# Attention maxima turned on VectorE and carried through DRAM, in a fused transformer block on one core

## The chip, the cores and the metric

The kernel runs on one core of one Trainium2 chip. The metric is the device time of one execution in microseconds. The time of a kernel is the median of several executions. One execution is profiled by the hardware, and all the views in this document are views of that execution's trace.

The engines go by the names of the profile: PE is TensorE's matmul stream and PEld its weight loads, DVE is VectorE, ACT is ScalarE, POOL is GpSimd, SP is SyncE. SP computes nothing here: it issues nearly all DMAs, one after the other, and SPq marks its instructions.

## The reference

One block of a diffusion transformer on x of 16 batches x 256 tokens x 256 channels, with 16 heads of 16 channels each:

```
x  = x + gate_a * (softmax(q k^T * scale) v) W_proj     # self-attention of modulate(ln(x))
x  = x + (softmax(q_c k_c^T * scale) v_c) W_cproj       # cross-attention to a context of 256 tokens
x  = x + gate_m * gelu(modulate(ln(x)) W_mlp1) W_mlp2   # MLP with 1024 hidden channels
```

The shifts, scales and gates come from a conditioning vector for each batch. All is float32. What matters here is the softmax: for each head and each query token the kernel subtracts the largest score over the keys before the exponential, and the change touches the way that this maximum takes.

## The kernel before, in words

**Stages.** There are 16 self-attentions ("s") and 16 cross-attentions ("c"), 32 *units* in all (`seq`, lines 725 to 740). Five s units come first, then s and c alternate, and the last are c. A setup stage (`PRE`, line 55) comes first and the MLP last. The change lies in the attention stage, which the trace shows from about 30 to 540 us.

**A unit has eight beats**, k = 0 to 7 (`beat`, lines 984 to 1136). All instructions are emitted in the order in which `beat` writes them (`InOrder`, line 40), and each engine's queue keeps that order. In beat k of unit n, `visit` (line 962) emits two things:

- for the *next* unit n+1, one piece of the scores in the orientation that the maximum needs: `s_tile` puts four `s` matmuls on PE, and one DVE reduction `mx<-s` takes the maxima of 4 heads x 128 query tokens (lines 640 to 666). After beat 3 the maxima of the unit's first 8 heads are complete (half 0), after beat 7 those of the other 8 (half 1).
- for the *current* unit n, one pair of heads in the transposed orientation: `t_part` puts four `st` matmuls on PE (line 676), and `exp` has ACT turn them into `pt` (line 687).

**How the maximum enters.** For each pair of heads the stacked tile `u.q` has 64 rows for each of two heads, and so has `u.k`. Row 63 of `u.q` holds minus the maximum of each query token, and row 63 of `u.k` holds a constant 1 (`ones`, line 88, sent by `one_rows`, line 884). So the `st` matmul over 64 rows gives score minus maximum; the `s` matmul uses 63 rows only.

**The way of a maximum** is `m_part` (line 668), once for each half of a unit, 64 times in all. The tile `mx` has query tokens on partitions and heads along a row. PE transposes 128 x 16 of it into a PSUM bank (`psm`), ACT multiplies by -1 into `m`, and one SP DMA (`big<-m`, 16 rows of 512 bytes) writes row 63 of both heads' rows of `u.q`. Half 1 of unit n is handled in beat 0 of unit n, after the `visit`, and is needed by the `st` matmuls of beat 4. Half 0 of unit n+1 is handled in beat 4 of unit n, after the `visit`, and is needed by the first `st` matmuls of unit n+1, in its beat 0. So each half has four beats.

**What else stands in SP's queue.** In beat 0 SP sends the new high parts of k (`big<-h_k` or `h_kc`, two DMAs of 256 KB), `big<-m`, and the low part `l_k`. In beat 1 come `S` and `U`, pieces of the attention output (`pull(1)`, line 573), and then the reciprocal row sums to DRAM (`rd<-S`, `spread`, line 584). In beat 4 come `h_q` twice, `big<-m` and `l_q`. In beat 5 a context load `c` may follow, and then `back` (line 588) reads the sums back, spread over all partitions (`R<-rd`, 256 KB). In beat 6 come the gates `g` (s units), `S` and `U` again (`pull(0)`), and a store.

Of the kernel before, what the change touches and what calls it, by code (L numbers as in the profile page):

```python
# [16 lines left out]
P = 128  # L17
# [4 lines left out]
def pixart_block(  # L22
# [29 lines left out]
                return tc.keep_in_program_order(i) if self.on else i  # L52
            return issue

    E_ = {'M': ((-17, -12, -5, -1, 1), (0, 3, 4, 7, 9), (8, 11, 13, 15)), 'LN': {'s': 'pool', 'c': 'pool', 'q': 'pool'}, 'ON': (1, 1, 1), 'H': (7, 11, 14, 15), 'AP': 23, 'DV': (0, 1), 'HP': (1, 0, 2), 'W1P': [(-9, 3), (-8, 3), (-7, 3), (-6, 3), (-4, 5), (-4, 7), (-3, 1), (-3, 5)], 'W2P': [(-4, 7), (-3, 2), (-3, 4), (-3, 6), (-3, 7), (-2, 2), (-2, 4), (-2, 6), (-1, 0), (-1, 1)], 'PRE': 'z0qp z0kp load ld2 ld3 rest one0 silu b12 brow L0a turn L0b b1 L0d scale hik lok T0t z1kp b2 shift T0h T0l ldm hiq loq hiv b1 K0a K0m L1a L1b lov L2a L2b bk z1qa bq K0h K0x K0ya L1e K0l K0s Q0a Q0m Q0h Q0x Q0ya T1t Q0l Q0s T1h V0a V0b T1l bv L2c L3a L3b L3p L3c K1a K1b', 'SL': {(-1, 0): 'Q1a Q1b K1x K1y K1l K1s', (-1, 1): 'T2t T2h T2p V1a Q1x Q1y Q1l Q1s', (-1, 2): 'V1b cpm2', (-1, 3): 'rest z2ka', (-1, 4): 'M0 rest one1 ld4', (-1, 5): 'K2a vone', (-1, 6): 'K2m z2qa', (-1, 7): 'rest one2', (0, 0): 'cpm0 d2 rest', (0, 1): 'rest', (0, 4): 'rest', (1, 0): 'rest', (1, 2): 'rest', (1, 4): 'rest'}}

    PE = InOrder(nc.tensor, True)
    ACT, DVE, POOL, SP = (InOrder(e, True) for e in (nc.scalar, nc.vector, nc.gpsimd, nc.sync))
# [9 lines left out]
    def ps_gen(name, tag=None):  # L68


        if tag is None and ps_turn[0] is not None:
            ps_turn[0] ^= 1
            tag = (SHORT, LONG)[ps_turn[0]]
        tag = tag or SHORT
        return psum.tile([P, 512], F32, tag=tag, name=name, bufs=2)
# [3 lines left out]
    DVE.memset(wz, 0.0)  # L79
    ident = const.tile([P, P], F32, name="ident")  # L80
    make_identity(nc, ident)
    mhalf = const.tile([P, 2], F32, name="mhalf")
    POOL.memset(mhalf, -0.5)

# [1 line left out]
    vts = [const.tile([P, NT, NH, 32], F32, name=f"v{i}") for i in range(3)]  # L86
    wself = const.tile([P, 16, H], F32R, name="wself")
    ones = const.tile([8, N], F32, name="ones")
    DVE.memset(ones, 1.0)


    BMOD, BQKV, BQC, BKVC, BM1 = 0, 12, 18, 20, 24
# [547 lines left out]
    def s_tile(u, g, par, t, bank=None, home=sp):  # L640

        alone = bank is None
        if alone:
            turn_of_s[0] ^= 1
            bank = turn_of_s[0]
        apart = isinstance(home, tuple)
        for j in range(2):
            PE.matmul((home[bank] if apart else home[:, bank])[:, j * N:(j + 1) * N],  # L650
                      u.q[par * 64:par * 64 + 63, 2 * g + j, t * P:(t + 1) * P],
                      u.k[par * 64:par * 64 + 63, 2 * g + j, :], start=True, stop=True)
            if j == 0:
                yield
        if u.mx is None:
            u.mx = work.tile([P, 2, 2, 4, NT], F32, tag="mx", name=f"mx_{u.n}", bufs=3)
        mx = u.mx.rearrange("p f r a t -> p r f a t")
        a = slice(2 * (g % 2), 2 * (g % 2) + 2)
        if alone or apart:
            src = home[bank] if apart else sp[:, bank]  # L660
            DVE.tensor_reduce(mx[:, par, g // 2, a, t], src.rearrange("p (j n) -> p j n", j=2),
                              AX.X, ALU.max)
        elif bank == 1:
            DVE.tensor_reduce(mx[:, :, g // 2, a, t], home.rearrange("p r (j n) -> p r j n", j=2),
                              AX.X, ALU.max)
        yield

    def m_part(u, hf):

        pst = ps_gen(f"psm_{u.n}_{hf}", SHORT)  # L670
        PE.transpose(pst[:16, :P], u.mx[:, hf].rearrange("p r a t -> p (r a t)"), ident)
        m = work.tile([16, P], F32R, tag="m", name=f"m_{u.n}_{hf}", bufs=1)
        ACT.mul(m, pst[:16, :P], -1.0)
        SP.dma_start(u.q[63:P:64, 4 * hf:4 * hf + 4, :].bitcast(F32), m.bitcast(F32))

    def t_part(u, pair, par):

# [16 lines left out]
    def exps():  # L694

        for f in later:
            f()
        later.clear()
# [234 lines left out]
    for k, f in zip("abpc", (u3.ln[0].steps[0], lambda: u3.ln[0].steps[1](False), u3.ln[0].pow, u3.ln[0].steps[2])):  # L933
        word["L3" + k] = f
    word["ldm"], word["cpm0"], word["cpm2"] = f_mod_load, lambda: f_mod(0), lambda: f_mod(2)
    word["M0"] = lambda: m_part(u0, 0)
    word["rest"] = lambda: next(rest, None)
    word["vone"] = lambda: [POOL.memset(v[:, :, :, 1:2 * HD:2], 1.0) for v in vts]
    for n, f in (("load", f_load), ("silu", f_silu), ("turn", f_turn), ("brow", f_brow),
# [44 lines left out]
    def beat(n, k):  # L984
# [20 lines left out]
        if k == 6:  # L1005
            if q2 and not n:
                q2.V.keep()
            if p2 and not alone:
                p2.end()
        visit(n, k)  # L1010
        if k == 0:
            if cur:
                m_part(cur, 1)
            exps()
            if q3 and q3.ready:
                q3.T[0].place()
            if prev:
                av_part(prev, 3)
            if q3 and q3.ready:
                q3.T[0].turn((0,))  # L1020
            if q2:
                q2.K.low()
                q2.K.send_low()
            if p2:
                p2.norm()
                p2.high()
                p2.low()
        elif k == 1:
            exps()
            run(lanes(q2 and q2.Q, q2 and n and q2.V))  # L1030
            if prev:
                p1.pull(1)
            if lc:
                lc.ln[0].steps[0]()
            if lx:
                if lx.b in (0, B - 1):
                    lx.ln[1].steps[0]()
                lx.ln[1].steps[1]()
                lx.ln[1].steps[2]()
        elif k == 2:  # L1040
            exps()
            if cur:
                av_part(cur, 0)
            if q3:
                q3.T[0].turn((1,) if q3.ready else (0, 1))
            if ls:
                ls.ln[0].steps[0]()
            elif prev:
                p1.recip()
                p1.spread()  # L1050
            if not (q3 and q3.kind == "c"):
                spare(n)
        elif k == 3:
            if q3:
                q3.T[0].high()
                if q3.kind == "c":
                    q3.T[0].full()
            exps()
            if alone and p2:
                p2.proj(0)  # L1060
                p2.proj(1)
            elif n:
                run(lanes(p2, q2 and q2.Q))
            else:
                run(lanes(q2.V, q2.Q))
            if q3 and q3.kind == "s":
                q3.T[0].low()
            if prev and ls:
                p1.recip()
                p1.spread()  # L1070
        elif k == 4:
            if nxt and lx:
                m_part(nxt, 0)
            exps()
            if nxt and not lx:
                m_part(nxt, 0)
            if alone:
                p2.end()
            if cur:
                av_part(cur, 1)  # L1080
            if lx:
                lx.T[1].turn()
            if q2:
                q2.Q.low()
                q2.Q.send_low()
            if q3 and q3.kind == "c":
                q3.T[0].rest_pool()
                spare(n)
            if ls:
                ls.ln[0].steps[1]()  # L1090
                ls.ln[0].steps[2]()
                ls.ready = True
        elif k == 5:
            exps()
            run(lanes(q3 and q3.K, (None if alone else p2) if n else q2.V))
            if cur:
                o_out(cur, 0)
            if lc:
                lc.ln[0].steps[1]()
                lc.ln[0].steps[2]()  # L1100
                lc.ready = True
            v = unit(n + 5)
            if v and v.kind == "c":
                load(v)
            if prev:
                p1.back()
        elif k == 6:
            exps()
            if lx:
                lx.T[1].high()  # L1110
            if cur:
                cur.post.begin()
                av_part(cur, 2)
                cur.post.pull(0)
            if q3 and p2:
                q3.vk = lanes(q3.V, q3.K)
                run(q3.vk, 1)
            if p3:
                p3.store()
            if lx:  # L1120
                lx.T[1].full()
                lx.T[1].rest_pool()
        elif k == 7:
            exps()
            run(q3.vk if q3 and p2 else lanes(q3 and q3.V, q3 and q3.K))
            if late:
                p2.add()
                p2.added = True
            elif lc:
                lc.ln[1].steps[0]()  # L1130
            v = unit(n + 5)
            if v and v.kind == "s":
                load(v)
            if n == nu - 1:
                p2.add()
                p2.store()
# [99 lines left out]
```

## Time and profile before

| what | value |
|---|---|
| median of 3 executions (lowest, highest) | 743.61 us (742.79, 745.01) |
| the profiled execution: its own time, its span | 742.45 us, 740.7 us |
| instructions in the trace | 22556 |
| busy over the span: PE, DVE, ACT, POOL | 722.2, 569.4, 556.1, 528.5 us |
| granted TensorE clock | 0.999 |
| DMA: packets, bytes | 81388, 106.15 MB |
| of `m_part`: PE transposes, ACT scalings, DMAs | 64 each |

The span runs from the first to the last instruction of the program; the execution's own time is 1.75 us longer. The views used below are: the page; stretches of time with each engine's busy time; the rows of one tile; instructions in order of time (start, duration, engine, operation, out<-in, and in brackets the idle time before and what ended it); and the chain of work that ended last, in order of time.

### The profile page before, as it was taken

What the parts mean: (1) busy time and instruction counts of PE and PEld (TensorE: products, weight loads), DVE (VectorE), ACT (ScalarE), POOL (GpSimd) and SP (SyncE); (2) the same over time, 40 slices, a digit from 0 to 9 for tenths busy, and PEclk for the clock granted to TensorE, in tenths of its full rate; (3) what the DMA queues carried; (4) which work ended last, traced back from release to release, by engine and by line L of the source; (5) the groups of instructions that cost most, each with busy time, mean ns of one, the idle gap of its engine ahead of it and who ended that gap; (6) DMA issues with size and microseconds to landing.
All of it is one profiled execution on the core that took longest, in us unless ns stands there. A gap on an engine that the chain in (4) does not pass through costs nothing.

```text
span 740.7 us, 22556 instructions
## 1 busy us (share of the span) xinstructions
PE 722.2 (98%) x9003; PEld 598.4 (81%) x9003; DVE 569.4 (77%) x882; ACT 556.1 (75%) x972; POOL 528.5 (71%) x525
## 2 busy tenths in 40 slices
PE   9999999999999999999999999999899999999997
PEld 8677777777777777777777787776479999999997
DVE  4778888878888887878788878778766877777762
ACT  5567888888888888887888888887766666666663
POOL 8465678797866868777686899985757676665663
PEclk9999999999999999999999999999999999999999
DMA  8365455544445455454555645545323132231311
GB/s 269 128 217 171 146 169 172 177 163 167 162 144 192 153 182 197 141 161 161 187 173 171 204 151 196 166 149 181 111 76 101 58 86 65 64 87 44 86 53 48
DMA packets 81388, 106.15 MB, mean 143 GB/s; under 512 B 16450, under 2 KB 44388, under 8 KB 81284
## 3 DMA queue, kind: packets, MB, share of 16 engines
q1 hardware_dynamic: 80180, 103.92, 43.3%
q8 instruction: 71, 1.16, 0.7%
q10 hardware_dynamic: 1104, 0.79, 0.4%
q14 instruction: 33, 0.27, 0.1%
HBM read 35.89 MB, written 8.98 MB: 61 GB/s over the span
## 4 chain that ended last, share of the span: by engine, by line
PE 92%; DVE 3%; ACT 2%; DMA 1%; issue 1%; POOL 1%; SPq 0%; ACTq 0%; POOLq 0%
PE s L51 18%; PE o L51 16%; PE st L51 14%; PE ph L51 13%; PE ps_P_s L51 4%; PE ps_k L51 3%; PE ps_v_s L51 3%; PE ps_kc L51 3%; PE ps_qc L51 3%; PE ps_v_c L51 2%; PE ps_q L51 2%; PE ps_P_c L51 2%; DVE mx L51 2%; PE psm L51 2%; PE psT_c L51 2%; PE psT_s L51 1%
## 5 line engine op out<-in xcount | busy, mean ns | idle before, releaser
L51 DVE TENSOR_REDUCE mx<-s 128x4 f32<-128x1024 f32 x252 | 307.7, 1221 | 89.2 <-PE s L51 88.7
L51 ACT ACTIVATE pt<-st 128x1024 f32<-128x1024 f32 x256 | 262.3, 1024 | 62.3 <-PE st L51 62.0
L51 PE MATMUL o<-pt,v 128*32 128x256 f32 x2048 | 137.1, 385 | 0.0
L51 PE MATMUL s<-big 63*128 63x256 f32 x1008 | 119.1, 307 | 5.5 <-DVE mx L51 4.0
L51 PE MATMUL st<-big 64*128 64x256 f32 (+1 forms) x1040 | 109.5, 284 | 3.1 <-ACT pt L51 1.7
L51 POOL TENSOR_TENSOR hl<-hf,hh 128x512 fp32r<-128x512 f32 x64 | 84.3, 1335 | 28.1 <-ACT hh L51 28.1
L51 PEld LDWEIGHTS s<-big 63*128 63x128 f32 x1008 | 79.0, 185 | 30.4 <-DVE mx L51 16.1
L51 PEld LDWEIGHTS st<-big 64*128 64x128 f32 (+1 forms) x1040 | 82.7, 186 | 6.6 <-ACT pt L51 3.4
L51 PEld LDWEIGHTS o<-pt,v 128*32 128x32 f32 x2048 | 53.4, 109 | 38.5
L51 ACT ACTIVATE hf<-ph,bT 128x256 f32<-128x256 f32 x120 | 50.4, 473 | 27.9 <-PE ph L51 27.9
L51 ACT ACTIVATE hh<-ph,bT 128x256 fp32r<-128x256 f32 x120 | 50.5, 472 | 20.9 <-PE st L51 9.8
L51 PE MATMUL ph<-wqch,wself 128*128 128x256 f32 x256 | 51.8, 286 | 1.3 <-ACT hh L51 1.3
L51 PE MATMUL ph<-wkch,wself 128*128 128x256 f32 x256 | 51.8, 286 | 0.0
L51 DVE TENSOR_SCALAR xn_m<-x,mv_m,rs_m 128x256 f32<-128x256 f32 x32 | 38.4, 1239 | 16.0 <-POOL rs_m L51 16.0
L51 PE MATMUL s<-big,hh 128*128 128x256 f32 x256 | 45.3, 276 | 0.0
L51 PE MATMUL st<-big,hh 128*128 128x256 f32 x256 | 45.0, 276 | 0.0
L51 PEld LDWEIGHTS ph<-wqch,wself 128*128 128x128 f32 x256 | 41.9, 191 | 1.9 <-ACT hh L51 1.5
L51 PEld LDWEIGHTS ph<-wkch,wself 128*128 128x128 f32 x256 | 41.9, 191 | 0.3
L51 POOL TENSOR_SCALAR xn_q<-x,mv_q,rs_q 128x256 f32<-128x256 f32 x32 | 38.9, 1225 | 1.7
L51 POOL TENSOR_SCALAR xn_c<-c,mv_c,rs_c 128x256 f32<-128x256 f32 x32 | 38.9, 1225 | 1.7
L51 PEld LDWEIGHTS s<-big,hh 128*128 128x128 f32 x256 | 38.8, 188 | 0.0
L51 PEld LDWEIGHTS st<-big,hh 128*128 128x128 f32 x256 | 38.8, 188 | 0.0
(214 smaller groups left out, 2215.7 us busy)
## 6 DMA issues: line engine op xcount, KB each, us to landing
big<-h_kc SPq DMA_DIRECT2D x32, 256.0 KB
big<-h_qc SPq DMA_DIRECT2D x32, 256.0 KB
big<-h_k SPq DMA_DIRECT2D x31, 256.0 KB
big<-h_q SPq DMA_DIRECT2D x31, 256.0 KB
big<-l_k SPq DMA_DIRECT2D x16, 256.0 KB
big<-l_q SPq DMA_DIRECT2D x16, 256.0 KB
g<-gd SPq DMA_DIRECT2D x16, 256.0 KB
U_s<-oT SPq DMA_DIRECT2D x32, 128.0 KB
```

What stands on the lines that cost most here:

```text
L51: i = f(*a, **k)
```

## The change

The transposition on PE, the scaling on ACT and the PSUM bank go. In their place VectorE transposes each 32 x 32 block of `mx` within itself (`DVE.transpose`, 128 x 32 to 128 x 32). That leaves the four blocks of 32 tokens in four groups of partitions, so the result goes to a scratch tile in DRAM (`md`, 16 KB, half of it the unused columns) by one DMA, and a second DMA (`m_send`) reads it back in pieces of 32 tokens, 128 bytes each, into the two rows 63 of `u.q`. The sign moves into the constant row, which becomes -1. The `mx` tiles are two constant tiles, zeroed once.

The first step, `m_part`, moves ahead of `visit` in beats 0 and 4. The second, `m_send`, stands two beats later: in beat 2 for half 1, and in beat 6 for half 0, each behind the exponential of that beat.

```diff
@@ (a schedule word for the first unit: in beat 6 ahead of it) @@
-(-1, 6): 'K2m z2qa'
+(-1, 6): 'm0 K2m z2qa'
...
     make_identity(nc, ident)
+    maxima = [const.tile([P, 2, 32], F32, name=f"mx{i}") for i in range(2)]
+    for t in maxima:
+        DVE.memset(t, 0.0)
...
-    DVE.memset(ones, 1.0)
+    DVE.memset(ones, -1.0)
...
         if u.mx is None:
-            u.mx = work.tile([P, 2, 2, 4, NT], F32, tag="mx", name=f"mx_{u.n}", bufs=3)
-        mx = u.mx.rearrange("p f r a t -> p r f a t")
+            u.mx = maxima[u.n % 2]
+        mx = u.mx[:, :, :16].rearrange("p f (r a t) -> p r f a t", r=2, a=4)
...
     def m_part(u, hf):
-        pst = ps_gen(f"psm_{u.n}_{hf}", SHORT)
-        PE.transpose(pst[:16, :P], u.mx[:, hf].rearrange("p r a t -> p (r a t)"), ident)
-        m = work.tile([16, P], F32R, tag="m", name=f"m_{u.n}_{hf}", bufs=1)
-        ACT.mul(m, pst[:16, :P], -1.0)
-        SP.dma_start(u.q[63:P:64, 4 * hf:4 * hf + 4, :].bitcast(F32), m.bitcast(F32))
+        mT = work.tile([P, 32], F32, tag="m", name=f"m_{u.n}_{hf}", bufs=2)
+        DVE.transpose(mT, u.mx[:, hf])
+        u.md = dram.tile([P, 32], F32, name=f"md_{u.n}_{hf}", bufs=2)
+        SP.dma_start(u.md, mT)
+
+    def m_send(u, hf):
+        SP.dma_start(u.q[63:P:64, 4 * hf:4 * hf + 4, :].bitcast(F32).rearrange("r a (t b j) -> r (a t) b j", t=NT, b=4),
+                     u.md.rearrange("(b r x) j -> r x b j", b=4, r=4)[0:2])
...
+        if k == 0:
+            m_part(cur, 1)
+        if k == 4 and nxt:
+            m_part(nxt, 0)
         visit(n, k)
         if k == 0:
-            if cur:
-                m_part(cur, 1)
             exps()
...
         elif k == 2:
             exps()
+            m_send(cur, 1)
...
         elif k == 4:
-            if nxt and lx:
-                m_part(nxt, 0)
             exps()
-            if nxt and not lx:
-                m_part(nxt, 0)
...
         elif k == 6:
             exps()
+            if nxt:
+                m_send(nxt, 0)
```

More of the change, by code (lines that the diff above doesn't have):

```diff
@@ L53, in __getattr__ @@
             return issue
-    E_ = {'M': ((-17, -12, -5, -1, 1), (0, 3, 4, 7, 9), (8, 11, 13, 15)), 'LN': {'s': 'pool', 'c': 'pool', 'q': 'pool'}, 'ON': (1, 1, 1), 'H': (7, 11, 14, 15), 'AP': 23, 'DV': (0, 1), 'HP': (1, 0, 2), 'W1P': [(-9, 3), (-8, 3), (-7, 3), (-6, 3), (-4, 5), (-4, 7), (-3, 1), (-3, 5)], 'W2P': [(-4, 7), (-3, 2), (-3, 4), (-3, 6), (-3, 7), (-2, 2), (-2, 4), (-2, 6), (-1, 0), (-1, 1)], 'PRE': 'z0qp z0kp load ld2 ld3 rest one0 silu b12 brow L0a turn L0b b1 L0d scale hik lok T0t z1kp b2 shift T0h T0l ldm hiq loq hiv b1 K0a K0m L1a L1b lov L2a L2b bk z1qa bq K0h K0x K0ya L1e K0l K0s Q0a Q0m Q0h Q0x Q0ya T1t Q0l Q0s T1h V0a V0b T1l bv L2c L3a L3b L3p L3c K1a K1b', 'SL': {(-1, 0): 'Q1a Q1b K1x K1y K1l K1s', (-1, 1): 'T2t T2h T2p V1a Q1x Q1y Q1l Q1s', (-1, 2): 'V1b cpm2', (-1, 3): 'rest z2ka', (-1, 4): 'M0 rest one1 ld4', (-1, 5): 'K2a vone', (-1, 6): 'K2m z2qa', (-1, 7): 'rest one2', (0, 0): 'cpm0 d2 rest', (0, 1): 'rest', (0, 4): 'rest', (1, 0): 'rest', (1, 2): 'rest', (1, 4): 'rest'}}
+    E_ = {'M': ((-17, -12, -5, -1, 1), (0, 3, 4, 7, 9), (8, 11, 13, 15)), 'LN': {'s': 'pool', 'c': 'pool', 'q': 'pool'}, 'ON': (1, 1, 1), 'H': (7, 11, 14, 15), 'AP': 23, 'DV': (0, 1), 'HP': (1, 0, 2), 'W1P': [(-9, 3), (-8, 3), (-7, 3), (-6, 3), (-4, 5), (-4, 7), (-3, 1), (-3, 5)], 'W2P': [(-4, 7), (-3, 2), (-3, 4), (-3, 6), (-3, 7), (-2, 2), (-2, 4), (-2, 6), (-1, 0), (-1, 1)], 'PRE': 'z0qp z0kp load ld2 ld3 rest one0 silu b12 brow L0a turn L0b b1 L0d scale hik lok T0t z1kp b2 shift T0h T0l ldm hiq loq hiv b1 K0a K0m L1a L1b lov L2a L2b bk z1qa bq K0h K0x K0ya L1e K0l K0s Q0a Q0m Q0h Q0x Q0ya T1t Q0l Q0s T1h V0a V0b T1l bv L2c L3a L3b L3p L3c K1a K1b', 'SL': {(-1, 0): 'Q1a Q1b K1x K1y K1l K1s', (-1, 1): 'T2t T2h T2p V1a Q1x Q1y Q1l Q1s', (-1, 2): 'V1b cpm2', (-1, 3): 'rest z2ka', (-1, 4): 'M0 rest one1 ld4', (-1, 5): 'K2a vone', (-1, 6): 'm0 K2m z2qa', (-1, 7): 'rest one2', (0, 0): 'cpm0 d2 rest', (0, 1): 'rest', (0, 4): 'rest', (1, 0): 'rest', (1, 2): 'rest', (1, 4): 'rest'}}
     PE = InOrder(nc.tensor, True)
@@ L935, in pixart_block @@
     word["ldm"], word["cpm0"], word["cpm2"] = f_mod_load, lambda: f_mod(0), lambda: f_mod(2)
-    word["M0"] = lambda: m_part(u0, 0)
+    word["M0"], word["m0"] = lambda: m_part(u0, 0), lambda: m_send(u0, 0)
     word["rest"] = lambda: next(rest, None)
```

## The prediction

> **What bounds the kernel now.** I read the page first, then one stretch of 100 us in the middle of the attention stage, then the chain of waits there, because the change lies in that stage only. The page:
>
> ```profile
> span 740.7 us, 22556 instructions
> PE 722.2 (98%) x9003; PEld 598.4 (81%) x9003; DVE 569.4 (77%) x882; ACT 556.1 (75%) x972; POOL 528.5 (71%) x525
> PE 92%; DVE 3%; ACT 2%; DMA 1%; issue 1%; POOL 1%; SPq 0%; ACTq 0%; POOLq 0%
> ```
>
> The stretch from 200 to 300 us (busy us and instructions of PE, PEld, DVE, ACT, POOL; granted clock, share of the DMA engines, GB/s):
>
> ```profile
> 200.00:300.00 100.00, 99.77 (x1456) 77.11 (x1453) 82.32 (x126) 83.12 (x132) 74.55 (x75) 1.00 0.50 167
> ```
>
> PE carries 92% of the chain and is busy 99.77 of 100 us; DVE and ACT have about 17 us free in 100. So PE's order of work sets the time, and one PE instruction less in a beat is worth what it takes there. What it takes is read from the chain (start, us, what), not from the pipelined duration:
>
> ```profile
> 196.19 0.21 PE psm L51
> ...
> 204.33 0.27 PE psm L51
> ...
> 211.96 0.21 PE psm L51
> ...
> 220.10 0.21 PE psm L51
> ```
>
> The four are beat 0, 4, 0, 4 of two units in a row: 0.21 us each, 0.27 once.
>
> **What goes.** The PE transposition and the ACT scaling, 64 of each (ns least, median, most):
>
> ```profile
> L51 PE MATMUL psm<-ident,mx x64: 269/277/278, 28.9 to 532.3; 128*16 128x128 f32 x64
> L51 ACT ACTIVATE m<-psm x64: 249/266/268, 30.7 to 532.7; 16x128 fp32r<-16x128 f32 x64
> ```
>
> On PE, 31 transpositions in beat 0 at 0.21 us are 6.5 us, and as many in beat 4 are 6.5 us more. ACT's 64 x 0.266 = 17 us lie on an engine with room, so I count them at nothing.
>
> **What DVE gets.** 64 transpositions of 128x32. The trace of before has none; the nearest rows (busy, mean ns, idle before) are a smaller and a slower instruction:
>
> ```profile
> L51 DVE TENSOR_REDUCE mx<-s 128x4 f32<-128x1024 f32 x252 | 307.7, 1221 | 89.2 <-PE s L51 88.7
> L51 DVE RECIPROCAL S_s<-S_s 128x32 f32<-128x32 f32 x16 | 5.6, 348 | 4.1 <-DMA S_s<-oT 3.2 <-DMA U_s<-oT 0.6
> L51 DVE BATCH_NORM_AGGREGATE mv_c<-st_c 128x2 f32<-128x6 f32 x32 | 3.8, 160 | 0.0
> ```
>
> Between 0.16 and 0.35 us each, so 10 to 22 us of DVE; I take 0.2, nearer to the small one, since 32 columns are few beside the 1024 that take 1.22. Each stands ahead of an `mx` reduction. DVE sits idle 88.7 us waiting for the `s` matmuls that those reductions read, and this cover hides it, except where DVE is late itself:
>
> ```profile
> 203.32 0.87 DVE L51 SCALAR_TENSOR_TENSOR xTl_s<-psT_s,sc,xTh_s 128x256 fp32r<-128x256 f32 x2
> 204.10 1.21 DVE L51 TENSOR_REDUCE mx<-s 128x4 f32<-128x1024 f32 x1
> ```
>
> ```profile
> 205.53 0.30 PEld L51 LDWEIGHTS s<-big 63*128 63x128 f32 x4 [0.41 <-DVE mx L51]
> ```
>
> This is beat 4 of every other unit: `xTl_s` runs straight into the reduction, which ends at 205.31, and PE's next `s` starts at 205.53. There the saving of 0.21 is used up by a reduction that starts 0.2 later. So without any new wait the change gives 6.5 us (beat 0) and, in beat 4, half of 6.5: about 10 us, at most 13.
>
> **What the new way of the maximum costs.** It has one SP issue in the place of `big<-m` and one more two beats later. Issues cost (ns) 0.58 us for `big<-m` and 0.32 for a write of 128 pieces of 128 bytes to DRAM, `rd`, which is `md`'s shape:
>
> ```profile
> L51 SPq DMA_DIRECT2D big<-m x64: 565/582/592, 30.9 to 533.0; - x64
> L51 SPq DMA_DIRECT2D rd_s<-S_s x16: 320/321/348, 60.9 to 458.2; - x16
> ```
>
> SP has the room. What matters is the wait: the first `st` matmul of a unit needs the second DMA, and PE keeps its order, so all PE work behind it, then DVE and ACT, wait with it. SP's queue and the `st` rows of two units:
>
> ```profile
> 205.99 0.58 SPq L51 DMA_DIRECT2D big<-m  x1
> ...
> 207.70 0.66 SPq L51 DMA_DIRECT2D R_s<-rd_s  x1
> 208.42 0.57 SPq L51 DMA_DIRECT2D S_c<-oT  x1
> ...
> 216.11 0.49 SPq L51 DMA_DIRECT2D U_c<-oT  x1
> ...
> 221.74 0.59 SPq L51 DMA_DIRECT2D big<-m  x1
> ...
> 223.69 0.65 SPq L51 DMA_DIRECT2D R_c<-rd_c  x1
> 224.39 0.44 SPq L51 DMA_DIRECT2D g<-gd  x1
> ```
>
> ```profile
> 211.55 0.40 PE L51 MATMUL st<-big 64*128 64x256 f32 x4
> ...
> 219.60 0.50 PE L51 MATMUL st<-big 64*128 64x256 f32 x4
> ...
> 227.73 0.41 PE L51 MATMUL st<-big 64*128 64x256 f32 x4
> ```
>
> Today `big<-m` goes out at 205.99 and is needed at 211.55: 5.56 us. In the changed kernel `md` takes that place, and `m_send` takes the place right behind `R`, at 208.42 and 224.39. That leaves 3.13 us in the first unit and 3.34 in the second. How long may it take? The lower bound is a small DMA with little ahead of it, `S_s` (64 pieces of 128 bytes):
>
> ```profile
> 199.49 0.60 SPq L51 DMA_DIRECT2D S_s<-oT  x1
> ```
>
> ```profile
> 201.45 0.35 DVE L51 RECIPROCAL S_s<-S_s 128x32 f32<-128x32 f32 x1
> ```
>
> The reciprocal that needs it ran 1.96 us after its issue. At that price `md` lands ahead of `m_send`'s place (205.99 + 1.96 = 207.95), and `m_send` lands 1.2 us early. The upper bound is the DMA directly ahead, `R`, 256 KB from DRAM, by its user on POOL:
>
> ```profile
> 211.85 1.28 POOL L51 TENSOR_TENSOR U_s<-U_s,R_s 128x512 f32<-128x512 f32 x1 [0.73 <-DMA R_s<-rd_s]
> ...
> 229.69 1.29 POOL L51 TENSOR_TENSOR U_c<-U_c,R_c 128x512 f32<-128x512 f32 x1 [1.74 <-DMA R_c<-rd_c]
> ```
>
> Its trips took 4.15 and 6.00 us. If `m_send` arrives with `R`, `st` starts 0.30 us late in the first unit and 1.96 us late in the second. Nor is that one pair an odd one:
>
> ```profile
> POOL U_c L51 <- DMA R_c<-rd_c: 13.5, 8, 3.9
> ...
> POOL U_s L51 <- DMA R_s<-rd_s: 6.5, 7, 1.8
> ```
>
> `R_c` was waited for 8 times, 1.7 us each, `R_s` 7 times, 0.9 us. I take the upper bound in the units behind `R_s` (0.30: the row directly ahead, same queue, same source, is the nearest), and 1.1 of the 1.96 us in those behind `R_c`, since only 8 waits of the 14 or so units show such a trip. That is 1.4 us for two units, 15 times: **21 us**. Both ends, 0 and 15 x 2.26 = 34 us, are kept for the range. The saving in beat 4 is lost where this wait decides: `R`'s issue hangs on `l_q` and SP's order, not on PE's beat 4. The saving in beat 0 stays, 6.5 us.
>
> The half sent in beat 2 has no `R` ahead: its place is behind `U_c`, at 216.60, and it is needed at 219.60. Of 3.00 us the lower price leaves 1.04, but the unit's `h`, `l` and `U` (768 KB and more) are ahead of it. I take nothing; a late third of 31 units at 0.5 us would be 5 us, kept for the upper end.
>
> [...]
>
> [...]
>
> **The sum.** 742.45 (the profiled execution, 1.16 under the median of 743.61) - 6.5 + 21 = 756.95, so **757 us**.
>
> **The rivals.**
>
> *No new wait* (faster). The decisive point is 3.1 us: if `m_send` lands within that of its issue, PE never waits for it, and only the transpositions' time is left, 742.45 - 10 = 732 (at most 13 us less: 729). For it speak the 1.96 us of `S_s` and that 8 KB is little; against it the place behind `R`, whose trips are 4 and 6 us. Chance 0.25.
>
> *Late with `R` in every unit, and late in beat 2 too* (much slower). 742.45 - 6.5 + 34 = 770, with beat 2's 5 us 775. For it: the DMAs behind `R` in the same queue, and the waits of up to 3.9 us above. Against it: half of the waits were short. Chance 0.24.
>
> *DVE takes PE's place.* With 0.35 us each, DVE gets 22 us more, at 82% of the stretch, and half of that would come in beats where it is late already: 742.45 - 13 + 11 = 740, up to 743 with a few waits. Or the small waits and the gain just cancel. Chance 0.06.
>
> That the change does not do what it says, a transposition that stays on PE, I see no way for: `psm` has no other source. Chance nil.
>
> **How the numbers follow.** The forecast, between 745 and 766, has 0.45. Slower by over 0.3% (2.2 us, about what a measurement of this kernel tells from none) has the forecast and the second rival: 0.69. Faster has the first and a part of the third, 0.26; within 0.3% the rest, 0.05. The range holds the first rival's 732 but not its end, and the second rival up to 776: 731 to 776. The forecast's own range is 745 to 766.
>
> **What would show it.** Right: PE rows `st` with idle time ended by a DMA `big<-md`, about 0.7 us a unit in the mean, nearly all at beat 0; the unit that ran from 211.55 to 227.73, 16.2 us, at about 17; PE busy under 97% of the middle stretch; no `psm`; `mx` idle longer. Wrong in the direction of the first rival: `st` rows without idle time and that unit at 15.8 us. Wrong for DVE: transposition rows of 0.3 us and `s` weight loads waiting for `mx`. What would make the forecast wrong above all is the trip of one DMA of 8 KB behind 256 KB, which no row of before shows.

## The result, and the profile after

| what | before | after |
|---|---|---|
| median (lowest, highest), 4 executions each | 743.20 us (742.79, 745.01) | 775.88 us (774.96, 785.02) |
| profiled execution: its own time, its span | 742.45, 740.7 us | 776.60, 774.8 us |
| granted TensorE clock | 0.999 | 0.980 |

The changed kernel takes 1.046 times as long (95% interval 1.038 to 1.054), 33 us more. The direction was forecast, with 14.5 us. Medians and ratios below leave out four disturbed executions: one of the kernel without the transposition (1692.6 us, the profiled one), one with dummy matmuls (790.9 us, the profiled one) and two of the last experiment (768.3 and 2324.9 us).

The page of the changed kernel, the lines that answer to those shown of before:

```profile
span 774.8 us, 22550 instructions
PE 730.1 (94%) x8939; PEld 603.8 (78%) x8939; DVE 577.6 (75%) x948; ACT 549.1 (71%) x908; POOL 529.2 (68%) x525
PE 60%; DMA 16%; DVE 10%; POOL 4%; issue 4%; SPq 3%; ACT 1%; ACTq 0%; DVEq 0%; POOLq 0%
```

The chain line is the one to look at first. PE's 92% fell to 60%, and DMA, with 1% before, carries 16%. So PE is no longer the only thing that sets the end. The same middle stretch (columns as in the prediction) tells how much of it is idle:

```profile
200.00:300.00 100.00, 95.55 (x1395) 73.93 (x1392) 80.62 (x135) 78.88 (x115) 72.91 (x74) 1.00 0.49 164
```

PE stands 4.45 us in 100 where it stood 0.23. Who it waits for, by the waits (us in total, times, longest):

```profile
PE st L51 <- DMA big<-md: 25.9, 22, 2.9
PEld s L51 <- DVE mx L51: 18.4, 28, 1.3
```

The first line is the forecast's wait. Here is how it looks in the unit with one of its longer trips: SP's queue, PE's `st` row, and the chain of the same stretch.

```profile
236.39 0.58 SPq L51 DMA_DIRECT2D md<-m  x1
...
238.35 0.99 SPq L51 DMA_DIRECT2D R_c<-rd_c  x1
240.10 0.53 SPq L51 DMA_DIRECT2D big<-md  x1
```

```profile
243.89 0.50 PE L51 MATMUL st<-big 64*128 64x256 f32 x4 [1.52 <-DMA big<-md]
```

```profile
236.39 3.69 DMA md<-m
240.09 0.02 issue
240.10 3.65 DMA big<-md
243.75 0.14 issue
243.89 0.50 PE st L51 x4
```

The chain runs through both trips and nothing else: 3.69 us to DRAM, 3.65 us back, then `st`. Over the 30 units that have an `R`, `m_send` is issued 0.76 us behind it in the median (the forecast used 0.72), and it lands within 1.0 us of `R`'s landing on either side, 0.2 us after it in the median.

DVE's transposition costs what was taken for it (ns least, median, most):

```profile
L51 DVE STREAM_TRANSPOSE m<-mx x64: 152/202/213, 30.7 to 567.1; 128x32 f32<-128x32 f32 x64
```

Something that the prediction did not name stands at the first unit. The first `st` row, and two stretches there (the column behind the five engines is the granted clock), after and then before:

```profile
37.98 0.80 PE L51 MATMUL st<-big 64*128 64x256 f32 x4 [2.60 <-DMA big<-md]
```

```profile
36.00:51.00 15.00, 13.02 (x86) 10.75 (x88) 5.86 (x9) 4.56 (x6) 1.88 (x2) 0.54 0.52 161
```

```profile
36.00:51.00 15.00, 14.68 (x200) 11.70 (x199) 11.95 (x19) 10.63 (x16) 7.00 (x8) 1.00 0.66 214
```

Both kernels keep PE busy over 13 of these 15 us, but the changed one does 86 matmuls and the one before 200. The clock was granted at half from 36.83 us on, for 13.65 us. The further falls lasted 6.83 us from 408.89, 6.83 from 548.83 and 3.41 from 565.90. The profiled execution of before has no such fall ahead of its end; others of that kernel had a granted clock of 0.989 to 1.000.

**Where the 34 us are.** Cutting both traces at the `st` rows of beats 0 and 4 of each unit, the end of the cut trace moves by 34.5 us: the first `st` is 3.07 us later, units 0 and 1 are 5.51 us longer, beats 4 to the next beat 0 of units 2 to 30 are 23.15 us longer, and beats 0 to 4 of units 2 to 31 are 2.79 us longer. In the last sum, three units with a half clock (22, 30, 31) hold +5.83 and all others -3.04.

### The profile page after: what moved, and what is told of

Same layout as the page of the kernel before. It is cut to its first block, busy times and chain, and to the rows that moved or that the text cites. A ratio compares the mean times of both kernels' runs of the same rounds, so it can differ in the third digit from the quotient of the medians.

```text
span 774.8 us, 22550 instructions
## 1 busy us (share of the span) xinstructions
PE 730.1 (94%) x8939; PEld 603.8 (78%) x8939; DVE 577.6 (75%) x948; ACT 549.1 (71%) x908; POOL 529.2 (68%) x525
## 4 chain that ended last, share of the span: by engine, by line
PE 60%; DMA 16%; DVE 10%; POOL 4%; issue 4%; SPq 3%; ACT 1%; ACTq 0%; DVEq 0%; POOLq 0%
PE ph L51 12%; PE s L51 12%; DMA big<-md 12%; PE st L51 11%; PE o L51 9%; DVE mx L51 5%; SPq L51 3%; PE ps_q L51 3%; PE ps_k L51 2%; PE ps_v_s L51 2%; DMA md<-m 2%; PE ps_qc L51 2%; PE ps_P_s L51 2%; PE psT_c L51 1%; POOL xn_q L51 1%
## 5 line engine op out<-in xcount | busy, mean ns | idle before, releaser
L51 PE MATMUL st<-big 64*128 64x256 f32 (+1 forms) x1040 | 114.7, 293 | 29.3 <-DMA big<-md 25.9
L51 PE MATMUL o<-pt,v 128*32 128x256 f32 x2048 | 141.0, 394 | 0.0
L51 PE MATMUL s<-big 63*128 63x256 f32 x1008 | 121.1, 311 | 6.8 <-DVE mx L51 6.3
L51 PEld LDWEIGHTS st<-big 64*128 64x128 f32 (+1 forms) x1040 | 85.2, 191 | 37.8 <-issue 15.1
L51 PEld LDWEIGHTS s<-big 63*128 63x128 f32 x1008 | 80.6, 189 | 33.5 <-DVE mx L51 18.4
L51 POOL TENSOR_SCALAR rs_c<-mv_c 128x2 f32<-128x2 f32 x16 | 3.7, 229 | 61.9 <-DVE mv_c L51 61.7
L51 ACT COPY oT<-o 128x512 f32<-128x512 f32 x64 | 37.4, 584 | 3.5 <-PE o L51 3.5
```

Of the source, the lines that this page charges most:

```text
L51: i = f(*a, **k)
```

## The experiments

My theory ahead of the runs was the prediction's own mechanism with the first unit added: the copy back is late because it stands behind `R`; the first unit costs a wait and the half clock that follows it. Rivals: the lateness comes from SP's order alone; from the way to DRAM; from sharing the DMA engines with anything; or from DVE. Each ratio is to executions of the kernel before on the same chip, taken beside it; us are medians.

**Without the copies back** (the maxima are never subtracted): the ceiling of what the change could give.

```diff
-            m_send(cur, 1)
-            if nxt:
-                m_send(nxt, 0)
```

> The second DMA (DRAM to the two rows of u.q) is left out for both halves of every unit; the DVE transposition and the first DMA stay. Part left out of the computation: the maxima are never subtracted (row 63 of u.q stays zero). Queue theory (PE waits because the second DMA stands behind R) and trip theory (PE waits because two DMAs in a row are simply too long, wherever they stand) both expect that all waits at the st matmuls go: 742.5 - 3 to -10, so 732 to 740 us, and a granted clock of 1.0 as before. If the clock's half-speed periods in the changed kernel are not caused by the waits, they stay, at 0.98, and the time is about 745.

Measured: 740.39 us, 0.9968 (0.9949 to 0.9987). Without any wait on DRAM the change is worth 2.4 us, not the 10 that the prediction gave it. The waits of before, and then of this kernel, say who takes the rest:

```profile
PEld s L51 <- DVE mx L51: 16.1, 30, 1.3
```

```profile
PEld s L51 <- DVE mx L51: 24.6, 45, 1.3
```

PE gives up its transposition and gets another wait for the maxima, 45 times instead of 30.

**Without the transposition too** (`m_part` emptied, nothing sent, maxima reduced and not used):

> Leaves out everything between the maxima and the score matmuls: no transposition on any engine, no copy to DRAM, no way back; the maxima are reduced and then not subtracted. Beside the run without the two copies back (740.4 us) it tells what VectorE's 64 transpositions and the copies to DRAM cost. Theory (the beats without the maxima's wait are bound by VectorE, so the transpositions of 0.2 us stand on the path): up to 64 x 0.2 = 13 us less, of which half lies in beats that wait, so about 733 to 736 us, and the groups of waits of the score weights on VectorE are smaller than 24.6 us. Rival (VectorE's idle time hides the transpositions, the limit is TensorE's own matmuls): within 1.5 us of 740.4.

Measured: 735.22 us, 0.9895 (0.9860 to 0.9931). So the whole way of the maximum by PE and ACT cost 7.8 us before, and DVE's transpositions with the copies to DRAM cost 5 us of that again.

**The kernel before with 64 idle transpositions on DVE:**

```diff
     def m_part(u, hf):
+        DVE.transpose(wz[:, :32], wz[:, :32])
```

> The kernel before, whole, and besides it one transposition of zeros by VectorE, 128 by 32 in place, at each of the 64 places of the maxima's transposition, of which nobody reads the result. Theory (VectorE is nearly as full as TensorE in the attention beats, so that 64 x 0.2 = 13 us of its work stand on the path for 4 to 6 us, as the two kernels without the copies back showed, 740.4 against 735.3 us): 746 to 750 us. Rival (VectorE's idle time hides them where TensorE's transposition still stands): within 1.5 us of the kernel before.

Measured: 745.83 us, 1.0034 (1.0008 to 1.0059), 2.2 us more. Between the two expectations: a cost is there, but a small one, and why it is smaller than the 5 us above was not tried. The profile shows waits for the idle transposition itself, but they hardly add to the waits of before (17.8 us in place of 16.1), and that execution, of 742.59 us, was no slower than before:

```profile
PEld s L51 <- DVE mx L51: 11.8, 20, 1.3
PEld s L51 <- DVE wz L51: 6.0, 13, 1.0
```

**`R` from ACT's queue,** so that SP's order holds no `R` ahead of the copy back:

```diff
-            SP.dma_start(o.R, o.rd...
+            ACT.dma_start(o.R, o.rd...
```

> R is issued by ACT's queue in the place of SP's; nothing else is changed. Queue theory: the second DMA for half 0 has no R ahead of it in SP's queue, its trip falls from about 4 us to about 2.2 us, the waits in beat 0 of units 2 to 30 (about 23 us) go or nearly go, and the two half-clock periods that follow long waits with them: 745 to 755 us. What stays is the wait of the first unit. Trip theory: the trip keeps its 3.6 to 4.2 us, time 770 us or more. If the transfers share what makes them slow and not the queue, the time lies between, 760 to 770.

Measured: 778.56 us, 1.0479 (1.0454 to 1.0504). Nothing gained. In one unit the two issues are 1.18 us apart on different queues, and `R` landed at 256.79 us and the copy back at 256.99; over the run the wait stays:

```profile
252.21 0.59 ACTq L51 DMA_DIRECT2D R_s<-rd_s  x1
253.39 0.55 SPq L51 DMA_DIRECT2D big<-md  x1
```

```profile
PE st L51 <- DMA big<-md: 20.9, 19, 2.8
```

The theory in its narrow form, the place in SP's queue, falls. What delays the copy is `R` in flight, by whichever queue: in 29 of the 30 units the copy went out as soon as `md` had landed, and it still arrived 0.9 us behind `R` in the median. The copy took 4.1 us in the median with `R` on the other queue, 3.8 in the changed kernel.

**Without `R`** (the load is left out, and the division by the row sums becomes a multiplication of `U` by itself):

> Leaves out the load of the reciprocal row sums R and the division by them (the multiplication by R becomes one of the same size of U by itself). Everything else of the changed kernel stays, the copy back of half 0 in beat 6 too. Theory (the 3.6 to 4.2 us of that copy come from R's transfer in flight ahead of it, by whichever queue R is issued): the copy takes about 2.1 us as it does where nothing stands ahead, the 23 us of waits ahead of beat 0 go, and the time comes to that of the order with the copy ahead of R, 751 us, or below by the R-free time of GpSimd: 746 to 752. Rival (the copy is late by its own issue in beat 6, by the first copy to DRAM or by the wide layout of its 128-byte pieces): 770 to 778 us, with the first score matmul of beat 0 still starting at the copy's landing.

Measured: 746.48 us, 1.0048 (1.0024 to 1.0071), inside the theory's span. The copy back of half 0 takes 2.2 us in the median instead of 3.8, with everything else in its place. What stays is the first unit and a few waits:

```profile
PE st L51 <- DMA big<-md: 5.6, 8, 2.5
```

**Half 0's copy back ahead of `R`:**

```diff
+            if nxt:        # beat 5
+                m_send(nxt, 0)
             if prev:
                 p1.back()
...
-            if nxt:        # beat 6
-                m_send(nxt, 0)
```

> The second DMA for half 0 is issued in beat 5 directly ahead of R, not in beat 6 behind it. Queue theory: its trip falls to about 2.2 us from an issue at about R's old place or when the first DMA lands, so beat 0 does not wait in most units; R goes out up to 1.5 us later, which its user on POOL mostly bears: 745 to 755 us. Trip theory: it is issued about 1.4 us earlier with the same trip of about 4 us, which takes away the wait where it was under 1.4 us: about 755 to 762, with trips still near 4 us in the trace.

Measured: 751.38 us, 1.0113 (1.0076 to 1.0150). One line's place gives 26 us back. The copy takes 2.2 us, and behind the first two units only two beats 0 wait for it, 0.17 and 0.42 us. Now beat 4 waits for half 1 in some units, because its way to DRAM was slow. In the unit with the longest of these waits, `md` issued at 401.09 landed at 406.64, and the copy back, first in line on SP, had to wait for it, and PE's `st` behind it for 2.02 us:

```profile
401.09 0.56 SPq L51 DMA_DIRECT2D md<-m  x1
...
406.66 0.56 SPq L51 DMA_DIRECT2D big<-md  x1
```

**Unit 0's first half by PE and ACT, all else as changed:**

```diff
-word["M0"], word["m0"] = lambda: m_part(u0, 0), lambda: m_send(u0, 0)
+word["M0"], word["m0"] = lambda: m_pe(u0, 0), lambda: None
```

> Only the first unit's half 0 goes back to the transposition on PE and one DMA. Clock theory (a wait of PE of 2.6 us at 35 us makes the granted clock fall to half for 13.65 us, and that costs more than the wait): the first half-clock period goes with the wait, the first st matmul is 2.6 us earlier and the first two units are 5 us shorter: 766 to 769 us, clock 0.99. If the wait alone counts: 773 us, and the half-clock period stays.

Measured: 779.21 us, 1.0484 (1.0422 to 1.0545). A miss: the first `st` was in time, but the wait moved to the unit's other half, whose copy stands behind weight loads in SP's queue, and the clock fell there, for 10.24 us from 45.75 on. PE's row of that wait in this run:

```profile
49.54 0.80 PE L51 MATMUL st<-big 64*128 64x256 f32 x4 [6.39 <-DMA big<-md]
```

**Dummy matmuls in the first wait:**

```diff
         in_turn(*s)
+        if (n, k) == (0, 0):
+            busy(12, ps_gen("ps_fill", SHORT))
         in_turn(*t)
```

> The changed kernel with 12 more matmuls on zeros between the weights and the score matmuls of unit 0's beat 0, where TensorE stood 2.6 us for the maxima and then ran at a granted clock of 0.5 for 13.65 us; nothing is left out. Theory (the clock fell because TensorE stood idle): no half clock between 36 and 51 us, unit 0 by 4 to 5.5 us shorter, the whole 770 to 773 us. Rival (the clock would have fallen anyway, by the load that the matmuls put on after a light stage): the half clock stays and the time is 776 us or some more. The later falls of the clock (409, 549 and 566 us) are touched by neither.

Measured: 781.80 us, 1.0512 (1.0465 to 1.0558). Missed as a time. In its profiled execution, of 790.9 us, the clock had already fallen at 10.9 us, so units started 6 us later. Locally, and in this one execution, the theory holds: the dummies fill the first wait and the clock stays full behind it, until the next wait, 3.99 us for the unit's second half. PE's rows in this run, and the stretches ahead of and behind the end of that wait (granted clock behind the five engines):

```profile
41.14 2.94 PE L51 MATMUL ps_fill<-wz 128*128 128x128 f32 x24
...
56.53 0.80 PE L51 MATMUL st<-big 64*128 64x256 f32 x4 [3.99 <-DMA big<-md]
```

```profile
44.00:55.00 11.00, 8.54 (x101) 7.17 (x100) 7.47 (x14) 5.66 (x8) 1.94 (x3) 1.00 0.61 184
55.00:63.00 8.00, 6.47 (x60) 4.90 (x60) 1.32 (x2) 2.86 (x4) 7.65 (x9) 0.57 0.39 137
```

**Copy ahead of `R`, and both halves of unit 0 by PE:** the diff of the copy ahead of `R`, and

```diff
+    def m_pe(u, hf):        # called for unit 0 in the places of before
+        pst = ps_gen(f"psm_{u.n}_{hf}", SHORT)
+        PE.transpose(pst[:16, :P], u.mx[:, hf, :16], ident)
+        m = work.tile([16, P], F32R, tag="y", name=f"m16_{u.n}_{hf}", bufs=1)
+        ACT.copy(m, pst[:16, :P])
+        SP.dma_start(u.q[63:P:64, 4 * hf:4 * hf + 4, :].bitcast(F32), m.bitcast(F32))
```

> The kernel with half 0's copy back ahead of R (751.4 us), and besides both halves of unit 0 by TensorE and ScalarE as before the change; nothing is left out. It tells the first unit's part from the rest. Theory (the clock falls to a half where TensorE has stood for over 2 us on a copy of the maxima in unit 0): no half clock between 35 and 60 us, the first score matmul at about 35 us, 743 to 746 us; the late copies of half 1 stay. Rival (the clock falls at the start of the scores whatever is done there): the half clock stays and the time is 749 us or more.

Measured: 748.18 us, 1.0067 (1.0033 to 1.0101). The first `st` is at 34.77 us, and the clock falls for 3.41 us from 53.8 on and again from 538.5. That is 3.4 us less than without it by the ratios, and less than expected: these falls and half 1's late copies remain.

**The copy to DRAM ahead of the sends of `h`,** alone:

```diff
+        if k == 0:
+            m_part(cur, 1)
+        if k == 4 and nxt:
+            m_part(nxt, 0)
         if k == 0 and q2:
             q2.K.high()
...
-        if k == 0:
-            m_part(cur, 1)
-        if k == 4 and nxt:
-            m_part(nxt, 0)
         visit(n, k)
```

> The changed kernel with one order changed: VectorE's transposition and the copy to DRAM ahead of the sends of h in beats 0 and 4, so that the maxima lie in DRAM 2 to 4 us earlier. The copy back of half 0 stays behind R, unit 0 stays on the new path; nothing is left out. Theory A (R's transfer itself delays the copy back, whenever the maxima have reached DRAM): the waits ahead of beat 0 stay, 770 to 780 us. Theory B (the copy back is late because its maxima reach DRAM late, so that it is issued behind R's packets; were it issued right behind R it would land in time): the waits ahead of beat 0 go, and the time is at or below that of the kernel with the copy ahead of R, 745 to 755 us. My prediction's step lies between the two: 0.3 us in half of the units and 1.1 in the other, 760 to 768 us.

Measured: 767.46 us, 1.0298 (1.0250 to 1.0347). The time lies in the span that the prediction's step would give, 760 to 768, and below theory A's, but the waits answer for theory A: with the maxima in DRAM in time (`md` issued 234.87, landed 236.37), the copy back still lands with `R`. They are smaller than in the changed kernel (25.9 us), so a part of those was `md` come late. The waits, SP's queue in one unit of this run, and its chain:

```profile
PE st L51 <- DMA big<-md: 18.8, 18, 2.6
```

```profile
238.18 0.66 SPq L51 DMA_DIRECT2D R_c<-rd_c  x1
238.93 0.53 SPq L51 DMA_DIRECT2D big<-md  x1
```

```profile
238.93 4.36 DMA big<-md
243.29 0.14 issue
243.42 0.50 PE st L51 x4
```

**Both orders changed:** the diffs of the copy ahead of `R` and of the copy to DRAM ahead of `h`.

> The changed kernel with both orders changed (the transposition and the copy to DRAM ahead of the sends of h, the copy back of half 0 ahead of R), unit 0 on the new path; nothing is left out. Beside the version with unit 0 by TensorE (737.6 us) it gives the first unit's price with no other wait left. Theory (the first unit's wait with the half clock behind it): 737.6 + 6 to 10 = 743 to 748 us, with a half clock of 10 to 14 us in the records between 35 and 52 us. Rival (the first unit's price is what two runs of different calls gave, 751.4 - 748.2 = 3.2 us): 739 to 742 us.

Measured: 744.90 us, 1.0000 (0.9975 to 1.0025). Against the next run, in which unit 0 goes by PE, the first unit's price is about 6 us (1.0000 and 0.9918). In this run the first `st` still waits 2.65 us, and the half clock behind it lasts 10.24 us.

**Both orders, and both halves of unit 0 by PE:** the same two, and unit 0 as above.

> Three orders changed at once, nothing left out: half 0's copy back ahead of R, the transposition and the copy to DRAM ahead of the sends of h in beats 0 and 4, and both halves of unit 0 by TensorE and ScalarE as before the change. Theory (what is left at 751.4 us with the copy ahead of R is the first unit's wait with its half clock, some 8 us, and the late copies of half 1, whose way to DRAM stands behind the sends of h, some 4 us): both go, and the time is that of the kernel with nothing sent back, 740.4, plus 0 to 4 us for the sends of h that now stand behind the transposition: 740 to 745 us. Rival (the DMA trips cost by sharing the engines with h, wherever they stand): 748 us or more, with h or the maxima's copies as releasers of the score matmuls.

Measured: 737.64 us, 0.9918 (0.9902 to 0.9934): faster than both kernels, and just below the expected span. The same middle stretch, and the wait that is left:

```profile
200.00:300.00 100.00, 99.14 (x1454) 76.63 (x1446) 84.14 (x139) 81.80 (x122) 75.41 (x75) 1.00 0.51 167
```

```profile
PEld s L51 <- DVE mx L51: 22.6, 42, 1.3
```

No `st` row waits for `big<-md` any more, and no fall of the clock stands ahead of 529 us. The sends of `h` behind the transposition cost nothing that shows.

**Straight from SBUF to SBUF,** four copies of 2 KB instead of one to DRAM and one back:

```diff
-        SP.dma_start(u.md, mT)
+        for b in range(4):
+            SP.dma_start(row[:, :, b], mT[32 * b:32 * b + 16])
```

> No scratch in DRAM: after VectorE's transposition four copies from SBUF to SBUF take the 4 blocks straight into the rows of q, at the place where the copy to DRAM is issued; the second trips of beats 2 and 6 go. Nothing is left out. Theory (the price of the change is the second trip, late behind R, and the first unit's): the rows land by about 4 us after the start of beats 4 and 0 and half a unit ahead of their use, all waits on them go but the first unit's (one trip less there), and the time is that of the kernel with nothing sent back, 740.4, plus 0 to 5 us for the first unit and its clock: 740 to 746 us. Rival (four issues instead of one hold SP's queue by about 0.6 us each, so that the sends of h behind them, and the matmuls on those, come late): 748 us or more, with the h loads as the releaser of TensorE.

Measured: 785.53 us, 1.0565 (1.0522 to 1.0608): the rival's case as a time, and no better than the change. The releaser is not the one that the rival named. The copies themselves take 1.6 us, but their four issues push the sums `S` back, and DVE, which keeps its order, waits for `S` with the maxima behind it:

```profile
216.90 2.28 SPq L51 DMA_DIRECT2D big<-m  x4
...
219.96 0.60 SPq L51 DMA_DIRECT2D S_s<-oT  x1
```

```profile
222.00 0.35 DVE L51 RECIPROCAL S_s<-S_s 128x32 f32<-128x32 f32 x1 [2.13 <-DMA S_s<-oT]
...
223.48 0.50 PE L51 MATMUL s<-big 63*128 63x256 f32 x4 [1.18 <-DVE mx L51]
```

**The same with half 1's four issues in beat 2, and unit 0 by PE:**

> No scratch in DRAM, as in the run with the direct copies (785.5 us), but the four copies of half 1 are issued in beat 2 and not in beat 0, and unit 0 goes by TensorE for both halves; nothing is left out. Theory (in that run the four issues of beat 0 held SP's queue, the sums S came late to VectorE's reciprocal and the maxima behind it, 1.3 to 2.8 us in nearly every first half of a unit): the first halves of the units come back to 8.0 us, and the time to 741 to 748 us. Rival (the pieces of 128 bytes slow the engines wherever they are issued): some other transfer comes late instead, 755 us or more.

Measured: 756.83 us, 1.0189 (1.0161 to 1.0218): the rival's time again. It is 28 us better by two changes at once, the place of four issues and unit 0 by PE (some 6 us above). `S_s` is still waited for, 18.4 us in 13 waits instead of 33.8 in 14. Half 0's four issues in beat 4 may push back what SP sends up to the next `S`; that was not tried.

## Why the prediction was wrong, point by point

The forecast added 14.5 us to the time (21 of waits, less 6.5 saved); the traces show 34.5. Its largest term, the new wait, was right. Three things failed beside it. The saving of 6.5 us came to 3.0, because DVE's idle time did not cover the transposition. The first unit (8.6 us) and the half clock (5.8 us) were not in the sum at all, and the prediction gives no reason for leaving them out.

The two orders make a table (ratio to before, and us more than before at 743.6):

| | `md` behind `h` | `md` ahead of `h` |
|---|---|---|
| copy back behind `R` | 1.0462, +34 (the change) | 1.0298, +22 |
| copy back ahead of `R` | 1.0113, +8 | 1.0000, 0 |

- **The new wait ahead of beat 0** (21 us): right in place, time of issue, landing and size. It measured 23.15 us in the profile. Behind `R_s` the waits were 0.47 us a unit (forecast 0.30), behind `R_c` 1.03 (1.1). That the total came so near is in part luck: the 1.1 was a choice between 0 and 1.96, and in five units the copy back was issued 1.3 to 2.6 us behind `R`, because `md` landed late there, which the sum had at nothing. With `md` ahead of `h` the same stretches are 18.63 us longer than before, not 23.15. The main cause is `R`'s transfer in flight, which moving `R` to ACT's queue does not cure (778.6) and taking `R` away does (746.5). The first rival needed a trip within 3.1 us. In 4 of 30 units the copy landed ahead of `R`, by up to 0.8 us, but the trip was still 3.8 us in the median, against 2.2 without `R`. The prediction's lower bound of a trip, the 1.96 us of `S_s`, was near that 2.2.
- **The saving in beat 0** (6.5 us): this step failed by half. It measured 3.0 us in the beats without a half clock. Even where no `st` waits for a copy the change gives 2.4 (1.0 - 0.9968) to 6.1 us (1.0 - 0.9918), where the prediction had 10, at most 13. The step "DVE's idle time hides the transposition" was the wrong one. The prediction saw that DVE is late itself in beat 4 of every other unit, and did not look at beat 0 of the units between. There DVE ran straight from `st_q` into the reduction before, and in the kernel without the copies back the reduction, now behind the transposition, holds PE's next `s` weights:

```profile
211.08 0.74 DVE L51 BATCH_NORM_STATS2 st_q<-x 128x6 f32<-128x256 f32 x2
...
211.76 1.23 DVE L51 TENSOR_REDUCE mx<-s 128x4 f32<-128x1024 f32 x1
```

```profile
210.56 0.19 DVE L51 STREAM_TRANSPOSE m<-mx 128x32 f32<-128x32 f32 x1
210.67 1.18 DVE L51 TENSOR_REDUCE mx<-s 128x4 f32<-128x1024 f32 x1
...
212.07 0.30 PEld L51 LDWEIGHTS s<-big 63*128 63x128 f32 x4 [0.17 <-DVE mx L51]
```

All twelve such units from the sixth to the twenty-eighth show this wait there, about 0.17 us each, and none of them did before. The price of 0.2 us was right, its cover was not.
- **ACT's 17 us at nothing**: no run speaks against it.
- **Half 1 in beat 2** (nothing taken, 5 us kept): little in the change itself, two waits at beat 4 of 1.43 and 0.24 us; that units which start late leave it time is likely, but not shown. As soon as `R`'s wait was gone, it cost: 11 us between 1.0067 and 0.9918, where beat 2's place is the same and only `md`'s place, behind `h` or ahead of it, differs.
- **The first unit** (not in the sum): 3.07 + 5.51 = 8.6 us in the profile, with a half clock in it; about 6 us with both orders changed, and 3.4 with the copy back alone ahead of `R`. The prediction's beats were those of the middle. The first `md` is issued at 30.9 us, and the `st` that needs it stood at 34.91 before: 4.0 us for two trips, where the prediction's middle unit had 5.56.
- **The half clock** (not in the sum): 5.8 us in three later units. The prediction read the clock of before, 0.999, as a given, though its own forecast added idle time on PE, and two of the four falls came in waits for a copy, 1.45 and 1.98 us in. Not all of it comes from waits for maxima: the kernels without the copies back and with both orders and unit 0 by PE each have a fall of 3.41 us too, from 529.86 and 529.13 on.

The surplus of 20 us over the forecast's sum is so made up of 3.5 (saving), 2.1 (wait), 8.6 (first unit) and 5.8 (half clock). The second rival named nearly the right time, 770 to 775, for a reason that the runs do not bear out: beat 2 was hardly late, and the wait behind `R` was not 34 us.

## What to carry to other kernels

When a value goes by DMA, look for a transfer in flight at its issue that lands late, on any queue, and issue the small one ahead of it: here the copy, 0.76 us behind `R`, landed within 1.0 us of it, and with `R` on ACT's queue it still came 0.9 us behind `R` in the median. Size alone does not tell. `R` landed 4.3 to 4.4 us after its issue in the median, the sends of `h` in beat 4, of 256 KB as well, after 2.5, and right behind two of those `md` took 2.0 us. What makes `R` slower than a send of `h` was not tried. Price the first unit by itself; a middle stretch does not show it. Before work is moved onto an engine with idle time, ask in which beats that idle time lies: here it stood where the other engine was late, and a part of the new work stood in the other beats.

## What the runs showed of the hardware that was not expected

The clock fell in the middle of waits of under 3 us. In the changed kernel PE's wait of 2.60 us had lasted 1.45 us when the clock fell at 36.83, and one of 2.90 us had lasted 1.98 when it fell at 408.89. The shortest half clock lasted 3.41 us, and the three later falls stand 109, 150 and 155 times 3.413 us behind the first. Cut into windows of that length that end at the falls, the trace shows PE busy for 1.25 to 2.00 us in the last window ahead of each of the four. Three of them, and one earlier window of the same grid, with a wait of 1.52 us and no fall behind it (PE's busy time stands first behind the length, the granted clock behind the five engines):

```profile
33.41:36.83 3.42, 1.61 (x12) 0.55 (x8) 2.94 (x5) 1.09 (x3) 1.92 (x4) 1.00 0.22 56
405.48:408.89 3.41, 1.43 (x24) 1.22 (x20) 3.03 (x5) 1.89 (x4) 1.29 (x1) 1.00 0.86 225
562.49:565.90 3.41, 2.00 (x28) 1.12 (x24) 2.81 (x3) 2.31 (x4) 2.81 (x4) 1.00 0.37 123
241.63:245.05 3.42, 1.90 (x32) 1.28 (x29) 2.40 (x5) 1.76 (x4) 2.21 (x3) 1.00 0.78 256
```

So the length of one wait does not tell: a fall came 1.45 us into one, and none came with a whole wait of 1.52 us. PE's busy time over the window does not tell either near 1.9 to 2.0 us of 3.41, where both outcomes are seen. What decides a fall is not shown. The last three of the four windows of the first half clock:

```profile
40.24:43.66 3.42, 3.42 (x20) 3.20 (x21) 1.42 (x2) 0.83 (x1) 1.41 (x2) 0.50 0.62 222
43.66:47.07 3.41, 3.41 (x28) 2.73 (x31) 1.25 (x2) 0.96 (x2) 0.00 (x0) 0.50 0.69 202
47.07:50.49 3.42, 3.42 (x30) 2.28 (x22) 1.24 (x3) 1.23 (x4) 0.00 (x0) 0.50 0.40 123
```

The half clocks of 3.41, 6.83, 10.24 and 13.65 us in these runs are one to four times 3.41 us. The windows ahead of the falls in the changed kernel were not idle throughout. Behind its first fall it took three windows with PE busy throughout before the clock came back, behind each of the other three falls one (PE busy 3.41, 3.40 and 3.41 us). What decides that number was not tried. Nor is it explained why the granted clock was between 0.7 and 0.8 in the first 20 us of the profiled executions with dummy matmuls and with the copies straight from SBUF to SBUF, and over 0.9 in that of the changed kernel.

A copy from SBUF to SBUF of 16 pieces of 128 bytes took 1.6 us in the median against 2.1 to 2.2 us for the 64 pieces of a half out of DRAM with nothing large ahead, yet the four copies of a half cost more than the trip that they spare: each issue took 0.52 us of SP's queue in the median.
